# Graph attention and a quantised feed-forward block in one launch: the residual written out early, the last products added by the DMA, SiLU in one instruction, two weight rows loaded sooner

## The chip, the cores and the metric

The kernel runs on one core of a Trainium2 chip, in one launch. The metric is the device time of the launch in microseconds (us). Engines are named as in the profile: PE (TensorE), DVE (VectorE), ACT (ScalarE), POOL (GpSimd), SP (SyncE, which here only issues DMAs).

## The reference

`x` is 384 x 1024, float32. The reference computes two residual blocks:

```python
x = x + GNN(layernorm(x))      # q,k,v = Linear; q2,k2,v2 = inner Linear of each; 16 heads of 64
                               # softmax(q2 k2^T / 8 + edge mask) v2, then Linear wo
x = x + FFN(layernorm(x))      # below

def FFN(x):                                   # 1024 -> 352 -> 1024
    xq   = fake_quant(x, clip_x)              # scale = sigmoid(clip) * max|x| / 127, over the WHOLE tensor
    gate = xq @ fq(w_gate).T                  # fq: int8 rows, scale = max|row| / 127
    up   = xq @ fq(w_up).T
    h    = fake_quant(silu(gate) * up, clip_down)   # again one scale for the whole tensor
    return h @ fq(w_down).T
```

The two maxima over a whole tensor are barriers: nothing can be quantised before the last element of the tensor is known.

## The kernel before, in words

The activations lie transposed in SBUF (features on the 128 partitions), in 8 blocks of 128 features. The work has these stages, with the profile's times from the start of the span:

1. **0 to 23 us**: load `x`, layernorm, transpose, first q columns. Edge lists become keys; POOL scatters edge weights into a mask in DRAM with 51 indirect DMAs until about 160 us.
2. **23 to 161 us**: `project2` (L178 to L226) makes q, k, v and the inner q with 7 block products instead of 8 per pair of output blocks, each of 4 matmuls (L189). One call is a round of some 9.1 us. DVE combines the products (L200 to L221) and prepares the weights of the next round (`left_sums`, L162 to L176; L171 makes `s2`, which the second product of the next round reads). `aside` feeds DVE one more piece after each product.
3. **161 to 318 us**: eight head pairs. In each, scores (L614), softmax on DVE and ACT (L620, L624, L634), transposes (L644), weighting by v (L652); between them PE takes work that doesn't depend on them: inner k and v, later the output projection.
4. **318 to 345 us**: output projection (L825), residual (`residual`, L757), second layernorm (`normalise`, L767), transposes (L866). The third block of 128 rows is the last; its row maxima go through `all_max` (L127, a transpose on PE and a reduction on DVE) into one scale (`act_scale`, L846).
5. **345 to 373 us**: quantise to int8 and back to bf16 (L894 to L897), gate and up matmuls (L906), SiLU (L912 to L918), maxima (L920), second scale (L930 to L933), quantise (L940 to L945), down products (L954, L958), residual and output (L962 to L967).

`ffn_weights` (L518) is a generator that loads, quantises and transposes the FFN weights, 14 rows of blocks. Two rows are loaded ahead; each step quantises one (L507 reduction, L508, L510, L513 on ACT, L515) and stops at its `yield`; the loop over head pairs takes one step at given places (`prepare`, L712). Its first step comes in `p = 0`.

**What sets the order.** PE, SP and POOL run in the order in which the code issues (`manual_schedule`, L74). DVE and ACT are in written order inside stages 1 and 2 (L266) and from L748 on; between them a scheduler places their instructions from its own estimates. Each engine executes in order, so an instruction that waits holds all behind it. SP's queue before the change, around stage 2's end: two `wik` rows, `biv_b` (L497), two `wiv` (L581), three `w_gate` rows (L528), then `w_up` rows that wait until ACT has freed a row buffer (`rows`, 3 buffers).

`keep_busy(n)` (L868) issues n transposes into a tile that nobody reads; it stands before each wait of PE in stages 4 and 5 (14, 14, 17 of them).

Of the kernel before, what the change touches and what calls it, by code (L numbers as in the profile page):

```python
# [23 lines left out]
F32 = mybir.dt.float32  # L24
# [8 lines left out]
P = 128  # L33
# [28 lines left out]
def gnn_ffn_kernel(ctx: ExitStack, tc: tile.TileContext, a: dict, out: bass.AP):  # L62
# [74 lines left out]
    mask = ffn.tile([P, NT, N], F32)  # L137
    nc.gpsimd.memset(mask, NO_EDGE)
    sig = ffn.tile([P, 2], F32)

    ident_b = const.tile([P, P], BF16)
    later = ph1.tile([P, GROUP * P], F32, name="later", bufs=1)
# [103 lines left out]
    with ph1_stack:  # L246
# [219 lines left out]
        for i, (name, o) in enumerate(todo[:-1]):  # L466
            (wa, wb), sums = wq_next, sums_next
            right, dst, cols = work[name]

            if name == "wq" and o == FIRST:  # L470
                aside = tables()
            elif name == "wiq" and o == KC - 2:
                aside = k_steps
            else:
                aside = islice(groups, GROUP + 1)
            wq_next = [load_w(todo[i + 1][0], todo[i + 1][1] + j) for j in range(2)]
            sums_next, steps = left_sums(*wq_next, turned if todo[i + 1][0] == "wik" else ph1)
            if name == "wv" and o == KC - 4:
                q_right, q_steps = right_sums(qT, ph1, "right")
                work["wiq"] = (q_right, q2, bias_of(3))  # L480
            if name == "wv" and o >= KC - 4:
                steps = in_turn(steps, islice(q_steps, 4))
            if name == "wiq" and o == KC - 4:
                k_right, k_steps = right_sums(kT, turned, "k_right")
                steps = in_turn(steps, islice(k_steps, 4))
            aside = in_turn(aside, steps)
            run(project2(
                wa, wb, sums, right, dst[:, o], dst[:, o + 1], cols[:, o : o + 1], cols[:, o + 1 : o + 2], ps_p, "p",
                lambda: next(aside, None),
            ))  # L490
            run(aside)
            if i == 0:
                nc.scalar.activation(sig, clip, AF.Sigmoid)
        run(groups)


    nc.sync.dma_start(biv_b, row_bcast(a["L0_gnn_biv"], F))  # L497
    ffn_w = ctx.enter_context(tc.tile_pool(name="ffn_w", bufs=1))
    wgT = ffn_w.tile([P, KC, I], BF16)
    wuT = ffn_w.tile([P, KC, I], BF16)  # L500
# [17 lines left out]
    def ffn_weights():  # L518

        units = [(name, m, ic) for m, name in enumerate(("L0_ffn_w_gate", "L0_ffn_w_up")) for ic in range(3)]  # L520
        units += [("L0_ffn_w_down", 2, c) for c in range(KC)]
        ahead = []

        def load_row():
            name, m, j = units[len(ahead)]
            i0, rows = ICS[j] if m < 2 else (j * P, P)
            wn = rows_p.tile([P, F], F32, name="row")
            nc.sync.dma_start(wn[:rows, : F if m < 2 else I], a[name][i0 : i0 + rows, :])  # L528
            ahead.append(wn)

        load_row()
        load_row()
        for u, (name, m, j) in enumerate(units):
            wn = ahead[u]
            if len(ahead) < len(units):
                load_row()
            if m < 2:
                i0, rows = ICS[j]
                wT = (wgT, wuT)[m]
                wq = quantise_rows(wn, rows, F, w_scale[:rows, m, j : j + 1])  # L540
                yield
                pt = ps_tp.tile([P, KC, P], BF16, name="tp")
                for k in range(KC):
                    nc.tensor.transpose(pt[:, k, :rows], wq[:rows, k * P : (k + 1) * P], ident_b[:rows, :rows])
                nc.scalar.copy(wT[:, :, i0 : i0 + rows], pt[:, :, :rows])
            else:
                wq = quantise_rows(wn, P, I, wd_scale[:, j : j + 1])
                yield
                pt = ps_tp.tile([P, 3, P], BF16, name="tp")
                for ic, (i0, rows) in enumerate(ICS):  # L550
                    nc.tensor.transpose(pt[:rows, ic, :], wq[:, i0 : i0 + rows], ident_b)
                nc.scalar.copy(wdT[:, 0:2, j * P : (j + 1) * P], pt[:, 0:2, :])
                nc.scalar.copy(wdT[:96, 2, j * P : (j + 1) * P], pt[:96, 2, :])

    with ExitStack() as ph:
        at = ph.enter_context(tc.tile_pool(name="at", bufs=4))
# [113 lines left out]
                    return  # L670

        NP = H // 2
        prep = ffn_weights()

        k2_next, first = inner_k(0)
        run(first)
# [90 lines left out]
        def normalise(t, last, st, hi, lo):  # L767
# [9 lines left out]
            nc.vector.tensor_scalar(above, hi[:, last : last + 1], hi[:, 0:1], mean, op0=ALU.max, op1=ALU.subtract)  # L777
            below = small.tile([P, 1], F32, name="below")
            nc.vector.tensor_scalar(below, lo[:, last : last + 1], lo[:, 0:1], mean, op0=ALU.min, op1=ALU.subtract)
            far = small.tile([P, 1], F32, name="far")  # L780
            nc.vector.tensor_scalar(far, below, -1.0, above, op0=ALU.mult, op1=ALU.max)

            r0 = small.tile([P, 1], F32, name="r2")
            nc.vector.reciprocal(r0, s0)
# [6 lines left out]
            if t == 0:  # L791
                nc.vector.tensor_mul(row_max[:, 0:1], far, rstd)
            else:
                nc.vector.tensor_scalar(
                    row_max[:, t : t + 1], far, rstd, row_max[:, t - 1 : t], op0=ALU.mult, op1=ALU.max
                )
            if t < NT - 1:

                minus = small.tile([P, 1], F32, name="minus")
                nc.vector.tensor_scalar(minus, mean, -1.0, None, op0=ALU.mult)  # L800
            for g in range(2):
                gs = slice(g * 512, (g + 1) * 512)
                if t < NT - 1:
                    nc.scalar.activation(xn[:, t, gs], x[:, t, gs], AF.Identity, bias=minus)
                    nc.scalar.activation(xn[:, t, gs], xn[:, t, gs], AF.Copy, scale=rstd)
                else:
                    nc.vector.tensor_scalar(xn[:, t, gs], x[:, t, gs], mean, rstd, op0=ALU.subtract, op1=ALU.mult)


        for t in range(NT):  # L810
# [7 lines left out]
            for g, (c0, width) in enumerate(groups):  # L818
# [11 lines left out]
                if 0 < g < len(groups) - 1:  # L830
                    nc.vector.tensor_tensor(hi[:, 0:1], hi[:, 0:1], hi[:, g : g + 1], op=ALU.max)
                    nc.vector.tensor_tensor(lo[:, 0:1], lo[:, 0:1], lo[:, g : g + 1], op=ALU.min)
            normalise(t, len(groups) - 1, st, hi, lo)
        run(prep)


    with ExitStack() as ph:
# [5 lines left out]
        hmx = small.tile([P, 4], F32, name="hmx")  # L843
        nc.gpsimd.memset(hmx, 0.0)

        def act_scale(mx, which):  # L846

            s = small.tile([P, 1], F32, name=f"as{which}")
            nc.vector.tensor_scalar(s, mx, sig[:, which : which + 1], 1.0 / QMAX, op0=ALU.mult, op1=ALU.mult)
            r = small.tile([P, 1], F32, name=f"ar{which}")  # L850
            nc.vector.reciprocal(r, s)
            return s, r

# [18 lines left out]
        turn(0)  # L874
        turn(1)
        keep_busy(14, ps_x, "x")

        idle = small.tile([P, 1], F32, name="idle")
        nc.scalar.activation(idle, clip[:, 0:1], AF.Sigmoid)
        sx, rx = act_scale(all_max(row_max[:, NT - 1 : NT], pt[:, :P]), 0)  # L880
        turn(2)
        keep_busy(14, ps_x, "x")
        gu_scale = small.tile([P, 2, 3], F32, name="gu_scale")
# [8 lines left out]
        for g in range(2):  # L892
            for t in range(2):
                nc.scalar.activation(part(x8, t, g), xnT[t][g], AF.Copy, scale=rx)  # L894
            nc.vector.tensor_scalar(part(x8, 2, g), xnT[2][g], rx, None, op0=ALU.mult)
            for t in (0, 2, 1):
                nc.vector.tensor_copy(part(xqT, t, g), part(x8, t, g))  # L897

        for col, ic, c0, width in ((0, 0, 0, N), (1, 1, 0, N), (2, 2, 0, N // 2), (3, 2, N // 2, N // 2)):
            i0, rows = ICS[ic]  # L900
            cs = slice(c0, c0 + width)
# [2 lines left out]
            for k in range(KC):  # L904
# [3 lines left out]
                    )  # L908
            sg = gu_scale[:rows, 0, ic : ic + 1]
            su = gu_scale[:rows, 1, ic : ic + 1]  # L910
            sgm = ff.tile([P, N], F32, name="sgm", bufs=2)
            nc.scalar.activation(sgm[:rows, :width], pg[:rows, :width], AF.Sigmoid, scale=sg)  # L912
            sl = ff.tile([P, N], F32, name="sl")
            nc.vector.scalar_tensor_tensor(
                sl[:rows, :width], pg[:rows, :width], sg, sgm[:rows, :width], op0=ALU.mult, op1=ALU.mult
            )
            nc.vector.scalar_tensor_tensor(
                hT[:rows, ic, cs], pu[:rows, :width], su, sl[:rows, :width], op0=ALU.mult, op1=ALU.mult  # L918
            )
# [8 lines left out]
            nc.scalar.copy(wd_scale_b[:, g * 512 : (g + 1) * 512], pt.rearrange("p a b -> p (a b)"))  # L928
        keep_busy(17, ps_x, "x")
        mx = small.tile([P, 1], F32, name="hmax")  # L930
        nc.vector.tensor_reduce(mx, hmx, axis=AX.X, op=ALU.max)
        pt = ps_tp.tile([P, P], F32, name="tp")
        sh, rh = act_scale(all_max(mx, pt), 1)  # L933

        h8 = ff.tile([P, 3, N], I8, name="h8", bufs=1)
        hq = ff.tile([P, 3, N], BF16, name="hq", bufs=1)
# [6 lines left out]
        for t in range(NT):  # L943
            ts = slice(t * P, (t + 1) * P)
            nc.vector.tensor_copy(hq[:, :, ts], h8[:, :, ts])  # L945
        last = []
        for t in range(NT):
            ts = slice(t * P, (t + 1) * P)
            for g in range(2):
# [6 lines left out]
                    )  # L956
                y = ff.tile([P, 512], F32, name="y", bufs=6)
                nc.vector.scalar_tensor_tensor(y, pm, sh, wd_scale_b[:, gs], op0=ALU.mult, op1=ALU.mult)  # L958
                if t * 2 + g >= 3:
                    last.append((t, gs, y))  # L960
                else:
                    nc.gpsimd.tensor_add(y, x[:, t, gs], y)  # L962
                    nc.sync.dma_start(out[t * P : (t + 1) * P, gs], y)

        for t, gs, y in last:
            nc.vector.tensor_add(y, x[:, t, gs], y)
            nc.sync.dma_start(out[t * P : (t + 1) * P, gs], y)  # L967


# [45 lines left out]
```

## Time and profile before

| | us |
|---|---|
| three runs | 373.28, 375.11, 375.08 (median 375.08) |
| the profiled execution | 374.68 |
| its span, first to last instruction | 372.9 |
| around the span | 1.78 |
| busy in the span: PE | 357.2 (96%) |
| DVE | 260.5 (70%) |
| ACT | 113.3 (30%) |
| POOL | 73.0 (20%) |
| TensorE clock granted, mean | 0.995 |

All times inside the kernel are counted from the span's start. "Idle before" in brackets is how long the engine stood before the instruction, and what released it. Matmul starts follow each other faster than their durations, since matmuls overlap. DMA rates are those of all 16 DMA engines of the core together.

### The profile page before, as it was taken

To read this page: it belongs to the slowest core of one execution; us is meant where nothing else is said; L and a number is where in the kernel's file an instruction comes from. 1 tells how busy PE (TensorE), PEld (TensorE's weight loads), DVE (VectorE), ACT (ScalarE), POOL (GpSimd) and SP (SyncE) were. 2 spreads that over 40 slices of the span, in tenths; PEclk is the share of its full clock that TensorE was granted. 3 is DMA by queue.
4 is the path that set the end of the run, shared out by engine and by line. 5 is a ranking of instruction groups with operands and counts; after the bars stand their busy time and mean duration, and the time that the engine had idled before them with its cause. 6 is when DMAs were issued, how large, how long until landed. Compare 5 with 4: busy or idle time off the path is not lost.

```text
span 372.9 us, 5877 instructions
## 1 busy us (share of the span) xinstructions
PE 357.2 (96%) x2112; PEld 298.4 (80%) x2113; DVE 260.5 (70%) x788; ACT 113.3 (30%) x270; POOL 73.0 (20%) x81
## 2 busy tenths in 40 slices
PE   7999999999999999899999999999999999999971
PEld 6999999999999999797886869687776545449660
DVE  5788888888889986998497367727583530199685
ACT  2242000000000000224573555536443524034330
POOL 6010354455445554300000000000000000000003
PEclk9999999999999999999999999999999999999998
DMA  7969433343333358257260040130394000000004
GB/s 232 394 221 394 135 115 113 116 134 114 113 115 114 113 171 253 74 156 233 56 227 3 19 134 19 53 138 0 131 376 130 5 0 2 0 0 3 1 2 169
DMA packets 17805, 44.52 MB, mean 119 GB/s; under 512 B 3262, under 2 KB 8400, under 8 KB 17392
## 3 DMA queue, kind: packets, MB, share of 16 engines
q1 hardware_dynamic: 15104, 39.46, 31.6%
q0 software_dynamic: 2672, 4.68, 4.1%
q8 instruction: 17, 0.28, 0.3%
q14 instruction: 12, 0.10, 0.1%
HBM read 41.91 MB, written 2.21 MB: 118 GB/s over the span
## 4 chain that ended last, share of the span: by engine, by line
PE 79%; DVE 9%; DMA 7%; ACT 2%; issue 1%; SPq 0%; DVEq 0%; ACTq 0%
PE p L189 34%; PE mm L189 8%; PE mm L591 8%; PE tp L644 4%; PE sc L614 3%; PE sc L652 3%; PE mm L662 3%; PE sc L662 3%; PE mm L825 3%; PE mm L306 3%; DMA row<-in_L_ffn_w_down_dram 3%; DMA row<-in_L_ffn_w_gate_dram 2%; DMA wt<-in_wq_dram 2%; PE sc L825 1%; DVE e L634 1%; DVE y L958 1%
## 5 line engine op out<-in xcount | busy, mean ns | idle before, releaser
L436 POOL DMA_INDIRECT mask_d<-value,place x51 | 57.5, 1128 | 64.9 <-DVE place L433 50.1
L189 PE MATMUL p<-actT,wt 128*128 128x192 f32 x360 | 65.8, 326 | 0.0
L189 PEld LDWEIGHTS p<-actT,wt 128*128 128x128 f32 x360 | 59.7, 190 | 0.0
L591 PE MATMUL mm<-wt,actT 128*128 128x256 f32 x192 | 46.1, 384 | 0.0
L591 PEld LDWEIGHTS mm<-wt,actT 128*128 128x128 f32 x192 | 34.8, 190 | 7.8 <-issue 2.2
L624 ACT ACTIVATE e<-s,mn 128x384 f32<-128x384 f32 x48 | 29.0, 606 | 26.8 <-DVE mn L620 26.7
L620 DVE CUSTOM_DVE_ANT_0 s<-sc,mask 128x384 f32<-128x384 f32 x48 | 24.5, 551 | 13.1 <-PE sc L614 13.0
L189 PE MATMUL p<-x_right,s 128*128 128x192 f32 x176 | 32.2, 326 | 0.0
L189 PE MATMUL p<-x_right,wt 128*128 128x192 f32 x176 | 32.2, 326 | 0.0
L842 POOL MEMSET hT<- 128x384 f32 x1 | 0.4, 418 | 156.9 <-PE sc L652 156.9
L189 PEld LDWEIGHTS p<-x_right,wt 128*128 128x128 f32 x176 | 29.2, 190 | 0.0
L189 PEld LDWEIGHTS p<-x_right,s 128*128 128x128 f32 x176 | 29.2, 190 | 0.0
L646 ACT COPY eTs<-tp 128x384 f32<-128x384 f32 x48 | 20.5, 478 | 25.5 <-PE tp L644 25.5
L423 DVE SCALAR_TENSOR_TENSOR junk<-key_b,key,later 128x384 f32<-128x384 f32 (+3 forms) x51 | 27.5, 539 | 0.0
L203 ACT COPY actT<-p 128x192 f32<-128x192 f32 x15 | 4.8, 318 | 66.1 <-PE p L189 66.1
L200 DVE SCALAR_TENSOR_TENSOR actT<-p,bias,actT 128x192 f32<-128x192 f32 x45 | 18.7, 415 | 8.4 <-PE p L189 6.6
L213 ACT ACTIVATE actT<-p,bias 128x192 f32<-128x192 f32 x15 | 6.3, 420 | 52.7 <-PE p L189 52.7
L644 PEld LDWEIGHTS tp<-ident,e 128*128 128x128 f32 x144 | 17.1, 141 | 5.0 <-issue 2.4
L644 PE MATMUL tp<-ident,e 128*128 128x128 f32 x144 | 19.7, 273 | 0.3 <-ACT eTs L646 0.3
L614 PE MATMUL sc<-k,actT 64*128 64x384 f32 x96 | 19.9, 518 | 0.0
L189 PE MATMUL mm<-actT,wt 128*128 128x192 f32 x96 | 18.9, 329 | 0.0
L634 DVE TENSOR_SCALAR e<-e,rs 128x384 f32<-128x384 f32 x48 | 17.2, 415 | 0.4
(215 smaller groups left out, 590.4 us busy)
## 6 DMA issues: line engine op xcount, KB each, us to landing
wt<-in_wq_dram SPq DMA_DIRECT2D x8, 512.0 KB, 11.4
wt<-in_wk_dram SPq DMA_DIRECT2D x8, 512.0 KB, 4.3
wt<-in_wv_dram SPq DMA_DIRECT2D x8, 512.0 KB, 4.3
wt<-in_wiq_dram SPq DMA_DIRECT2D x8, 512.0 KB, 3.9
wt<-in_wik_dram SPq DMA_DIRECT2D x8, 512.0 KB, 4.7
wt<-in_wiv_dram SPq DMA_DIRECT2D x8, 512.0 KB, 5.2
wt<-in_wo_dram SPq DMA_DIRECT2D x8, 512.0 KB, 7.6
actT<-in_x_dram SPq DMA_DIRECT2D x6, 512.0 KB, 4.2
```

Of the source, the lines that this page charges most:

```text
L189: nc.tensor.matmul(z, left[:, k * P : (k + 1) * P], r[:, k, :], start=(k == 0), stop=(k == HK - 1))
L200: nc.vector.scalar_tensor_tensor(dst, z, b, with_, op0=ALU.add, op1=ALU.add)
L423: nc.vector.scalar_tensor_tensor(junk[:, :left], keys[:, (c - k0) * P : (c - k0) * P + left], key[:, c : c + 1], later[:, :left], op0=ALU. ...
L436: ins = nc.gpsimd.indirect_dma_start(out=mask_d, out_offset=bass.IndirectOffsetOnAxis(ap=place[:, c : c + 1], axis=0), in_=value[:, c : c ...
L591: nc.tensor.matmul(pm, vT[:, k, t * P : (t + 1) * P], wt[k // HK][:, k0 : k0 + 256], start=(k == 0), stop=(k == KC - 1),)
L614: nc.tensor.matmul(ps[t, h], q2[hs, t * P : (t + 1) * P], k2[hs, :], start=True, stop=True)
L620: nc.vector.tensor_tensor_reduce(s, ps[t, h], mask[:, t, :], -SCALE, 3.0e38, op0=ALU.add, op1=ALU.min, accum_out=mn[h][:, t : t + 1],)
L624: nc.scalar.activation(e[h][:, t, :], s, AF.Exp, bias=mn[h][:, t : t + 1], scale=-1.0, accum_out=sm[h][:, t : t + 1],)
L634: nc.vector.tensor_scalar(e[h][:, t, :], e[h][:, t, :], rs[:, t : t + 1], None, op0=ALU.mult)
L644: nc.tensor.transpose(pt[:, t * P : (t + 1) * P], e[h][:, t, m * P : (m + 1) * P], ident)
L646: nc.scalar.copy(eT[h][m], pt)
L662: nc.tensor.matmul(pm, outT[:, k, t * P : (t + 1) * P], wo[k][:, gs], start=(k == 0), stop=(k == KC - 1))
```

## The change

Four parts; the names are those of the code.

- **FFN rows ahead of `wiv`**: a `yield` after the first two `load_row()`; the generator is made and advanced once before the head pairs, ahead of the load of `biv_b`. SP's queue becomes `wik`, `wik`, `w_gate` rows 1 and 2, `biv_b`, `wiv`, `wiv`, `w_gate` row 3. The scheduler places the first two reductions of gate rows about one round sooner on DVE.
- **Scales**: sigmoid(clip)/127 is made once on ACT, early (`per_max`), and multiplied into the row maxima in `normalise` (`size`, `far`) and, for the second scale, into the final reduction (`tensor_tensor_reduce` instead of `tensor_reduce`). `act_scale` goes: what `all_max` returns is the scale, and one reciprocal follows.
- **Last row block and SiLU**: of the third block, columns 0 to 511 are normalised on DVE after `row_max`, columns 512 to 1023 on ACT in two instructions. Of its two quantisations, one moves from DVE to ACT. `Sigmoid` on ACT and a product on DVE become one `Silu` on ACT, four times; the table load for it moves behind the quantisation.
- **Output**: SP writes `x` after the first residual to the output, six DMAs of 128 x 512, as soon as each part is final. The six additions (three on POOL, three on DVE) go; each product `y` is sent by POOL's queue with `accumulate add` onto the output.

```diff
@@ first round of project2
                 nc.scalar.activation(sig, clip, AF.Sigmoid)
+                nc.scalar.activation(per_max[:, 0:1], sig[:, 0:1], AF.Copy, scale=1.0 / QMAX)
+                nc.scalar.activation(
+                    per_max[:, 1:5], sig[:, 1:2].to_broadcast([P, 4]), AF.Copy, scale=1.0 / QMAX
+                )
...
-    nc.sync.dma_start(biv_b, row_bcast(a["L0_gnn_biv"], F))
@@ ffn_weights
         load_row()
         load_row()
+        yield
...
+    prep = ffn_weights()
+    next(prep)
+    nc.sync.dma_start(biv_b, row_bcast(a["L0_gnn_biv"], F))
...
-        prep = ffn_weights()
@@ normalise
+            size = small.tile([P, 1], F32, name="size")
+            nc.vector.tensor_scalar(size, below, -1.0, above, op0=ALU.mult, op1=ALU.max)
             far = small.tile([P, 1], F32, name="far")
-            nc.vector.tensor_scalar(far, below, -1.0, above, op0=ALU.mult, op1=ALU.max)
+            nc.vector.tensor_mul(far, size, per_max[:, 0:1])
+            if t == NT - 1:
+                minus = small.tile([P, 1], F32, name="minus")
+                nc.vector.tensor_scalar(minus, mean, -1.0, None, op0=ALU.mult)
...
-            for g in range(2):
+            for g in range(2) if t < NT - 1 else (1,):
                 gs = slice(g * 512, (g + 1) * 512)
-                if t < NT - 1:
-                    nc.scalar.activation(xn[:, t, gs], x[:, t, gs], AF.Identity, bias=minus)
-                    nc.scalar.activation(xn[:, t, gs], xn[:, t, gs], AF.Copy, scale=rstd)
-                else:
-                    nc.vector.tensor_scalar(xn[:, t, gs], x[:, t, gs], mean, rstd, op0=ALU.subtract, op1=ALU.mult)
+                nc.scalar.activation(xn[:, t, gs], x[:, t, gs], AF.Identity, bias=minus)
+                nc.scalar.activation(xn[:, t, gs], xn[:, t, gs], AF.Copy, scale=rstd)
+            return mean, rstd
@@ first scale
-        idle = small.tile([P, 1], F32, name="idle")
-        nc.scalar.activation(idle, clip[:, 0:1], AF.Sigmoid)
-        sx, rx = act_scale(all_max(row_max[:, NT - 1 : NT], pt[:, :P]), 0)
+        nc.vector.tensor_scalar(
+            xn[:, NT - 1, :512], x[:, NT - 1, :512], mean, rstd, op0=ALU.subtract, op1=ALU.mult
+        )
+        sx = all_max(row_max[:, NT - 1 : NT], pt[:, :P])
+        rx = small.tile([P, 1], F32, name="ar0")
+        nc.vector.reciprocal(rx, sx)
@@ quantise
-            nc.vector.tensor_scalar(part(x8, 2, g), xnT[2][g], rx, None, op0=ALU.mult)
-            for t in (0, 2, 1):
+            if g == 0:
+                nc.vector.tensor_scalar(part(x8, 2, g), xnT[2][g], rx, None, op0=ALU.mult)
+            else:
+                nc.scalar.activation(part(x8, 2, g), xnT[2][g], AF.Copy, scale=rx)
+            for t in ((2, 0, 1), (0, 1, 2))[g]:
                 nc.vector.tensor_copy(part(xqT, t, g), part(x8, t, g))
+        idle = small.tile([P, 1], F32, name="idle")
+        nc.scalar.activation(idle, clip[:, 0:1], AF.Silu)
+        for t in range(NT):
+            for g in range(2):
+                gs = slice(g * 512, (g + 1) * 512)
+                nc.sync.dma_start(out[t * P : (t + 1) * P, gs], x[:, t, gs])
@@ SiLU
-            nc.scalar.activation(sgm[:rows, :width], pg[:rows, :width], AF.Sigmoid, scale=sg)
...
-            nc.vector.scalar_tensor_tensor(
-                sl[:rows, :width], pg[:rows, :width], sg, sgm[:rows, :width], op0=ALU.mult, op1=ALU.mult
-            )
+            nc.scalar.activation(sl[:rows, :width], pg[:rows, :width], AF.Silu, scale=sg)
@@ second scale
-        nc.vector.tensor_reduce(mx, hmx, axis=AX.X, op=ALU.max)
+        nc.vector.tensor_tensor_reduce(
+            scaled, hmx, per_max[:, 1:5], 1.0, -3.0e38, op0=ALU.mult, op1=ALU.max, accum_out=mx
+        )
...
-        sh, rh = act_scale(all_max(mx, pt), 1)
+        sh = all_max(mx, pt)
+        rh = small.tile([P, 1], F32, name="ar1")
+        nc.vector.reciprocal(rh, sh)
@@ output
-                if t * 2 + g >= 3:
-                    last.append((t, gs, y))
-                else:
-                    nc.gpsimd.tensor_add(y, x[:, t, gs], y)
-                    nc.sync.dma_start(out[t * P : (t + 1) * P, gs], y)
-        for t, gs, y in last:
-            nc.vector.tensor_add(y, x[:, t, gs], y)
-            nc.sync.dma_start(out[t * P : (t + 1) * P, gs], y)
+                nc.gpsimd.dma_start(out[ts, gs], y, accum_op=ALU.add)
```

More of the change, by code (lines that the diff above doesn't have):

```diff
@@ L139, in gnn_ffn_kernel @@
     sig = ffn.tile([P, 2], F32)
+    per_max = ffn.tile([P, 5], F32)
     ident_b = const.tile([P, P], BF16)
@@ L832, in gnn_ffn_kernel @@
                     nc.vector.tensor_tensor(lo[:, 0:1], lo[:, 0:1], lo[:, g : g + 1], op=ALU.min)
-            normalise(t, len(groups) - 1, st, hi, lo)
+            mean, rstd = normalise(t, len(groups) - 1, st, hi, lo)
         run(prep)
@@ L844, in gnn_ffn_kernel @@
         nc.gpsimd.memset(hmx, 0.0)
[L846 to L852, printed above, removed]
         pt = ps_x.tile([P, 512], F32, name="x")
@@ L910, in gnn_ffn_kernel @@
             su = gu_scale[:rows, 1, ic : ic + 1]
-            sgm = ff.tile([P, N], F32, name="sgm", bufs=2)
-            nc.scalar.activation(sgm[:rows, :width], pg[:rows, :width], AF.Sigmoid, scale=sg)
             sl = ff.tile([P, N], F32, name="sl")
-            nc.vector.scalar_tensor_tensor(
-                sl[:rows, :width], pg[:rows, :width], sg, sgm[:rows, :width], op0=ALU.mult, op1=ALU.mult
-            )
+            nc.scalar.activation(sl[:rows, :width], pg[:rows, :width], AF.Silu, scale=sg)
             nc.vector.scalar_tensor_tensor(
@@ L930, in gnn_ffn_kernel @@
         mx = small.tile([P, 1], F32, name="hmax")
-        nc.vector.tensor_reduce(mx, hmx, axis=AX.X, op=ALU.max)
+        scaled = small.tile([P, 4], F32, name="hscaled")
+        nc.vector.tensor_tensor_reduce(
+            scaled, hmx, per_max[:, 1:5], 1.0, -3.0e38, op0=ALU.mult, op1=ALU.max, accum_out=mx
+        )
         pt = ps_tp.tile([P, P], F32, name="tp")
-        sh, rh = act_scale(all_max(mx, pt), 1)
+        sh = all_max(mx, pt)
+        rh = small.tile([P, 1], F32, name="ar1")
+        nc.vector.reciprocal(rh, sh)
         h8 = ff.tile([P, 3, N], I8, name="h8", bufs=1)
@@ L945, in gnn_ffn_kernel @@
             nc.vector.tensor_copy(hq[:, :, ts], h8[:, :, ts])
-        last = []
         for t in range(NT):
```

## The prediction

> **What bounds the kernel now.** I read the shares first, then the chain of waits, then the timeline around each place that the diff touches.
>
> ```profile
> PE 357.2 (96%) x2112; PEld 298.4 (80%) x2113; DVE 260.5 (70%) x788; ACT 113.3 (30%) x270; POOL 73.0 (20%) x81
> ```
>
> PE is busy 96% of the span, so up to 345 us only what makes PE stand still can be won. PE's own timeline between 100 and 345 us has three stops of over 0.3 us: 1.80 at 153.22, 0.52 at 192.16, 0.33 at 279.00. The largest, on PE and on DVE:
>
> ```profile
> 147.92 1.22 DVE L507 TENSOR_REDUCE wmx<-row 128x1 f32<-128x1024 f32 x1 [1.55 <-DMA row<-in_L_ffn_w_gate_dram]
> ...
> 150.54 1.22 DVE L507 TENSOR_REDUCE wmx<-row 128x1 f32<-128x1024 f32 x1 [0.28 <-DMA row<-in_L_ffn_w_gate_dram]
> ...
> 152.48 0.68 DVE L171 TENSOR_TENSOR s<-s,wt 128x512 f32<-128x512 f32 x1
> ...
> 153.22 1.57 PE L189 MATMUL p<-right,s 128*128 128x192 f32 x8 [1.80 <-DVE s L171]
> ```
>
> DVE stood for two gate rows, L171 behind them came late, and PE stood for L171. In the last stage the chain of waits goes over DVE and PE in turn, and ends so:
>
> ```profile
> 356.63 0.87 PE tp L927 x8
> 357.51 1.85 PE x L872 x17
> 359.36 0.14 PE tp L129
> 359.50 0.02 issue
> 359.53 0.30 DVE allmax L131
> 359.83 0.03 issue
> 359.86 0.22 DVE as L849
> ```
>
> The 17 fillers of L872, not the data, release L129 here. After the products the output DMAs remain. The table by stretch has, from 368 us on, the DMA share and GB/s as its last columns:
>
> ```profile
> 368.00:369.00 1.00, 0.00 (x0) 0.00 (x0) 0.47 (x1) 0.00 (x0) 0.00 (x0) 1.00 0.99 377
> 369.00:370.00 1.00, 0.00 (x0) 0.00 (x0) 0.00 (x0) 0.00 (x0) 0.00 (x0) 0.68 1.02 387
> 370.00:370.50 0.50, 0.00 (x0) 0.00 (x0) 0.00 (x0) 0.00 (x0) 0.00 (x0) 0.50 0.66 250
> 370.50:372.90 2.40, 0.00 (x0) 0.00 (x0) 0.00 (x0) 0.00 (x0) 0.00 (x0) 0.50 0.00 0
> ```
>
> The engines end at 368.47; the DMAs move data until 370.33 (0.66 of the third row) at 100% share and some 390 GB/s; 2.6 us of closing follow in any case.
>
> **Part 1, FFN rows ahead.** The first two gate rows were issued at 141.48 behind two `wiv` rows. Now they follow the `wik` rows, at about 132.4, where `biv_b` stood. `biv_b` landed 5.5 us after 132.42, at 137.9; gate row 1 takes that place, row 2 needs 512 KB at 390 GB/s more, 1.3 us: 139.2. In the new order of DVE the two reductions stand behind the L423 that ended at 137.41 and behind L218 some 3 us later, so they wait for data at most 0.5 us. They cost DVE the same 2 x 1.22, but a round sooner. I followed DVE's order from there with the durations of before: it runs some 2.5 us behind the old times at 142 us (the four PSUM buffers of L189 and the 3.5 us by which L171 is ahead in that round cover this), catches up in its old gaps, and ends L171 of the last round at 151.8 to 152.3, since gate row 3's reduction (1.20) still stands ahead of it. PE wants it at 151.42. The stop of 1.80 becomes 0.4 to 0.9: 0.9 to 1.4 won, I take 1.1.
>
> `w_up` rows then need not hold SP: the second one kept SP from 154.91 to 164.4, and the next `wik` with it (DVE waited 1.04 for that at 171.10). The third up row's reduction (1.22 at 173.92, between two L620) comes sooner, so the softmax and what follows on ACT are some 0.5 us earlier. That takes something from the stop of 0.52 at 192.16 and from two gaps of 0.18 at 166.50 and 169.39. I take 0.4 of these 0.88. Sum: **-1.5**. Bounds: -2.7 (all of 1.80 and 0.88), and +0.3, if the rows in flight share the DMA engines, gate row 1 lands at 139.5 and DVE carries another 1.6 us into the last round. `biv_b` moves to about 140.7; its reader L597 starts at 176.55. The mask's scatters move by 2 us; the mask is read at 173.24 and was back at 164.5.
>
> **Part 2, up to the first scale.** Each `normalise` gains one small DVE instruction on the way (0.16; by starts 0.2), the last one also `minus`: 0.24. For t = 0 and 1 the idle 0.34 ahead of 341.51 hides all but 0.07. Then only one L807 half (0.50) stands between `row_max` and L131, and L849 (0.24 by starts) goes. By starts, L131 begins at 345.22 instead of 345.30 and the reciprocal ends at 345.70 instead of 346.02. ACT makes the other half in two instructions of 0.72 from about 343.9 on, done at 345.3 to 345.6, when PE has finished the first four transposes. Quantisation started on ACT 0.38 after the reciprocal and is now five instructions at 0.58 by starts on ACT, with the casts behind it: the last cast ends at 349.5 instead of 349.88. PE, filled to 347.9, then runs on from 349.55 instead of 349.93: **-0.35** (bounds 0, if ACT's half is late, and -0.6, if those 0.38 vanish). The table load (1.28 at 343.04) moves behind ACT's quantisation, 349.1 to 350.4; SiLU's first input comes at about 350.9. The cover is 0.5 us; without it the load costs up to 0.8.
>
> **Part 3, SiLU and second scale.** The trace shows no Silu; I take Sigmoid's rows (0.58 and 0.42), same shape and engine. Four DVE products leave (0.62, 0.62, 0.41, 0.41), and the last maximum comes about 1.0 us sooner. That is worth **nothing**: the fillers on PE still end as late. Without the fillers it would be 1.0. The new reduction with its accumulator read (L759 at 128 wide: 0.30) hides there too. Behind L131, L849 leaves the path: **-0.24**. All products `y` are then 0.6 us earlier: the first ends at 362.3, the sixth at 365.6.
>
> **Part 4, output.** Off the path go three DVE additions (L966, 2.35 together) and three on POOL (1.27 each). The early writes are six DMAs on SP, whose queue is empty from 286.4 on; they start between 326 and 342 us, where the DMA engines move nothing, and land (2.1 us) 18 us ahead of the first addition. They cost nothing. The accumulating DMAs are issued by POOL, each behind its `y`. An issue on POOL takes 0.54 (L257) to 0.80 (L450), about the 0.66 between two `y`; from L450's issue to its first data were 1.5 us. First data: 362.3 + 0.1 + 1.5 = 363.9. Then six transfers at a price p each, which no row shows:
>
> - p = 0.67, a plain write (256 KB at 390 GB/s): end 367.9, against 370.33: -2.4. Less is excluded, as the write rows are at full share.
> - p = 1.34, if fetching the old output costs as much as a second transfer: end 371.9, +1.6.
> - p = 2.1, if each waits for the landing of the one before (the output's row, issue to landing): end 376.5, +6.2.
>
> The write row is the nearest, but its engines are at 100%, so the second read can't be free; reading and writing overlap in a plain DMA, so it need not cost all. I take 1.0, between the first two: end 369.9, **-0.4**.
>
> A page speaks against the change here. "Collectives: The Full Stack" of the Trainium skill, section "The bandwidth ceiling: the fold count and why AG ≠ RS ≠ AR", says that an addition inside a DMA reads two sources through the ring that limits it, and gives a measured ratio of 1.93 between plain and adding transfers. By that estimate p is 1.29 and the sum comes to 374.5. No run here shows it yet.
>
> **Sum.** Against the profiled execution, 374.68 (span 372.9 + 1.78): -1.5 from part 1, -0.4 from part 4, in which the 0.35 + 0.24 of parts 2 and 3 are contained: **372.8**. That execution lies 0.40 below the median of the three runs, 375.08.
>
> **Rivals.**
> - *The write price holds* (p = 0.67): -1.5 - 2.4, 370.8. For it: the DMA engines are idle until then, and the price is that of the rows at hand. Against it: full share with one read. Chance 0.25.
> - *The DMA takes back what the engines won* (p = 1.2 to 1.5): 374.0 to 375.8, at 1.34 374.8. POOL's and DVE's additions went, but the bytes that are read double. Chance 0.22.
> - *Slower: the additions in the DMA go one after the other.* Place: the 16 DMA engines after 363.9. Price: at p = 2.1, +6.2 - 1.5, 379.4. It ties at p = 1.32 and is slower by over 0.5% (377.0) from 1.70. For it: nothing else may touch a destination between its read and write. Against it: each DMA is 128 separate rows over 16 engines, which need not wait for each other. Chance 0.08.
> - *The gate rows don't land in time* (part 1 worth +0.3 to -0.5): 373.8 to 374.6. Against it: rows in one queue landed one after another here (6.4, 8.5, 8.6 us after issue). Chance 0.05.
>
> **Numbers.** The forecast, p of 0.85 to 1.2 with part 1 as taken, has 0.40. The range goes from 370.5 (write price, part 1 at -1.8) to 375.9 (p = 1.34, part 1 at -0.4). A measurement here tells about 0.5% from no change, that is 373.2 and 377.0: the first rival and three quarters of the forecast lie below, 0.56; the serial rival and the end of the second above, 0.12; 0.32 between.
>
> **What would show it.** Part 1: PE's stop at 153 is under 1 us, and the gate rows' reductions on DVE wait for no DMA. Part 2: the first scale's reciprocal 0.3 earlier against the end of the last residual. Part 3: fillers still run into the transpose of `all_max` with DVE idle before its reduction. Part 4: the DMA share stays near 1 after the last `y`; six transfers divided by that time give p. I am wrong if p is outside 0.85 to 1.2, if POOL's issues are over 0.66 apart, or if Silu or its table load delays the first maximum.

## The result and the profile after

| | before | after |
|---|---|---|
| median of 4 runs, us | 375.1 | 380.61 |
| ratio, 95% interval | | 1.0152 (1.0122 to 1.0182) |
| profiled execution | 374.68 | 380.61 |
| its span | 372.9 | 378.9 |
| first `y` ends | 362.91 | 362.52 |
| first output data | 365.10 | 364.35 |
| last output data (but for single packets, up to 370.4 and 374.6) | 370.33 | 374.4 |
| from there to the end of the span | 2.6 | 4.5 |

The forecast was 372.8, in a range of 370.5 to 375.9. The kernel became 1.5% slower. The shares of the profile after:

```profile
PE 358.7 (95%) x2112; PEld 298.9 (79%) x2113; DVE 255.0 (67%) x782; ACT 115.6 (31%) x275; POOL 78.0 (21%) x84
```

DVE works 5.5 us less and PE 1.5 us more: the engines do not show the loss. The table by stretch of the kernel after does (length, then busy time of PE, PEld, DVE, ACT, POOL; PE's clock, DMA share and GB/s):

```profile
364.00:366.00 2.00, 0.99 (x5) 0.25 (x3) 1.81 (x3) 0.00 (x0) 2.00 (x4) 1.00 0.85 95
366.00:368.00 2.00, 0.00 (x0) 0.00 (x0) 0.00 (x0) 0.00 (x0) 2.00 (x3) 1.00 1.15 180
368.00:370.00 2.00, 0.00 (x0) 0.00 (x0) 0.00 (x0) 0.00 (x0) 0.28 (x1) 1.00 1.08 118
370.00:372.00 2.00, 0.00 (x0) 0.00 (x0) 0.00 (x0) 0.00 (x0) 0.00 (x0) 0.54 1.05 175
372.00:374.00 2.00, 0.00 (x0) 0.00 (x0) 0.00 (x0) 0.00 (x0) 0.00 (x0) 0.50 1.11 202
374.00:374.50 0.50, 0.00 (x0) 0.00 (x0) 0.00 (x0) 0.00 (x0) 0.00 (x0) 0.50 0.37 62
374.50:378.90 4.40, 0.00 (x0) 0.00 (x0) 0.00 (x0) 0.00 (x0) 0.00 (x0) 0.50 0.00 0
```

The DMA engines are full (share near 1 or above, as packets overlap), but move 95 to 202 GB/s where the plain writes moved some 390. Six blocks of 256 KB in the 10.05 us from 364.35 to 374.4 are 1.7 us each. The rate is not even: it is low until 366, and again, at 118 GB/s with full engines, from 368 to 370. Then 4.5 us pass in which no engine and no DMA works. The end of the timeline after:

```profile
361.77 0.75 DVE L976 SCALAR_TENSOR_TENSOR y<-mm,allmax,wd_scale_b 128x512 f32<-128x512 f32 x1 [0.27 <-PE mm L972]
...
362.83 5.45 POOL L978 DMA_DIRECT2D out_dram<-y  x6 [16.40 <-DVE y L976]
```

The first `y` ends at 361.77 + 0.75 = 362.52, only 0.39 sooner than before. POOL needs 5.45 us for six issues, 0.91 each.

At the second maximum the order is as predicted. Fillers and transpose on PE, maximum and next reduction on DVE, from the timeline after:

```profile
357.21 2.02 PE L878 MATMUL x<-ident 128*128 128x128 f32 x17
...
357.83 0.08 DVE L946 DVE_READ_ACCUMULATOR2_ANT hmax<- 128x1 f32 x1
359.07 0.27 PE L129 MATMUL tp<-ident,hmax 128*128 128x128 f32 x1
359.38 0.29 DVE L131 TENSOR_REDUCE allmax<-tp 128x1 f32<-128x128 f32 x1 [1.47 <-PE tp L129]
```

SiLU brings the maximum to 357.9, and DVE then stands 1.47 us until the 17 fillers let the transpose go. SiLU's table load delays nothing: it ends at 350.59, and the first SiLU on ACT, at 351.20, has waited 0.39 for PE. Around the FFN rows, the first two reductions on DVE, L172 on DVE, and PE's stops of over 0.3 us in the kernel after:

```profile
138.99 1.22 DVE L512 TENSOR_REDUCE wmx<-row 128x1 f32<-128x1024 f32 x1 [1.50 <-DMA row<-in_L_ffn_w_gate_dram]
141.38 1.21 DVE L512 TENSOR_REDUCE wmx<-row 128x1 f32<-128x1024 f32 x1
152.04 0.68 DVE L172 TENSOR_TENSOR s<-s,wt 128x512 f32<-128x512 f32 x1
```

```profile
148.18 1.57 PE L190 MATMUL p<-actT,wt 128*128 128x192 f32 x8 [0.42 <-issue]
152.78 1.57 PE L190 MATMUL p<-right,s 128*128 128x192 f32 x8 [0.43 <-DVE s L172]
158.77 1.57 PE L190 MATMUL p<-actT,wt 128*128 128x192 f32 x8 [0.53 <-DVE wt L211]
167.21 1.57 PE L190 MATMUL mm<-k_right,wt 128*128 128x192 f32 x8 [0.37 <-DVE k L201]
```

The stop of 1.80 is 0.43 now. Three others of this size stand beside it that were not there: 0.42, 0.53 and 0.37.

To tell the stages apart over several traces I use four landmarks: PE in steady rounds near 100 us (100.55 in the kernel before), PE's first `wiv` products (170.79), the first transposes of the third block (341.31), and the start of the first `y` (362.16).

### The profile page after: what moved, and what is told of

It reads as the page before. It is cut to its first block, busy times and chain, and to the rows that moved or that the text cites. A ratio compares the mean times of both kernels' runs of the same rounds, so it can differ in the third digit from the quotient of the medians.

```text
span 378.9 us, 5878 instructions
## 1 busy us (share of the span) xinstructions
PE 358.7 (95%) x2112; PEld 298.9 (79%) x2113; DVE 255.0 (67%) x782; ACT 115.6 (31%) x275; POOL 78.0 (21%) x84
## 4 chain that ended last, share of the span: by engine, by line
PE 63%; issue 14%; DVE 10%; DMA 6%; ACT 3%; POOL 1%; POOLq 0%; SPq 0%; ACTq 0%
PE p L190 29%; PE mm L602 8%; PE mm L190 7%; PE tp L655 4%; PE sc L625 3%; PE sc L663 3%; PE mm L673 3%; PE mm L307 3%; DMA row<-in_L_ffn_w_down_dram 3%; PE sc L673 2%; DMA row<-in_L_ffn_w_gate_dram 2%; DVE wmx L512 1%; DVE e L645 1%; ACT w8b L518 1%; POOL out_dram L978 1%
## 5 line engine op out<-in xcount | busy, mean ns | idle before, releaser
L437 POOL DMA_INDIRECT mask_d<-value,place x51 | 60.8, 1191 | 64.9 <-DVE place L434 45.8
```

Of the source, the lines that this page charges most:

```text
L437: ins = nc.gpsimd.indirect_dma_start(out=mask_d, out_offset=bass.IndirectOffsetOnAxis(ap=place[:, c : c + 1], axis=0), in_=value[:, c : c ...
```

## The experiments

The theory after the result: the adding transfers cost 1.7 us each instead of 1.0, and the way they are sent lengthens the closing. The rivals: the loss comes from another part; or GpSimd's queue, not the addition, is what is slow.

**The output part alone.** The kernel before, with

```diff
+        for t in range(NT):          # ahead of the gate and up products
+            for g in range(2):
+                nc.sync.dma_start(out[t * P : (t + 1) * P, gs], x[:, t, gs])
...
-                    nc.gpsimd.tensor_add(y, x[:, t, gs], y)
-                    nc.sync.dma_start(out[t * P : (t + 1) * P, gs], y)
+                nc.gpsimd.dma_start(out[ts, gs], y, accum_op=ALU.add)
```

and the three additions of `last` gone.

> The kernel before with the output part alone (residual written early, six adding transfers on GpSimd's queue). Theory 1, the adding transfers are what costs: from the kernel after, data moves for 10.1 us after the first y (6 x 1.7) and 4.7 us of closing follow, against 7.4 and 2.6 in the kernel before; y comes 0.4 later than in the kernel after (362.9 against 362.5), so 381.0 us, ratio 1.016. Theory 2, the loss comes from the other parts (a later first y, hidden in my alignment of the two traces): within 1 us of the kernel before, 374 to 376.

Measured: 381.5, ratio 1.0164 (1.0135 to 1.0193). Its first `y` starts 20.87 us after the transposes, against 20.85 before: the early writes delay nothing. Data moves until 375.5, 12.0 us after the first `y` ended (7.4 before), and 4.4 us follow. The whole loss is in the output part. (With full engines, the rate here is 153 to 196 GB/s in each stretch of two microseconds from 366 to 374.)

**The FFN rows alone.**

```diff
-    nc.sync.dma_start(biv_b, row_bcast(a["L0_gnn_biv"], F))
...
         load_row()
         load_row()
+        yield
...
+    prep = ffn_weights()
+
+    next(prep)
+    nc.sync.dma_start(biv_b, row_bcast(a["L0_gnn_biv"], F))
...
-        prep = ffn_weights()
```

> The kernel before with the FFN rows ahead of wiv alone. Theory 1, VectorE is full from 142 to 170 us and now has six of the 1.2 us reductions there instead of five: PE's stop at 153 shrinks but others open at 148, 159 and 167, and PE starts L602's first group 0.5 to 0.7 later than before (171.3 to 171.5 on this scale) and is 0.5 later at 340 us; the span is 0.3 to 0.6 us longer, 375.0 to 375.3 for the profiled execution. Theory 2, my prediction's step: 1.5 shorter, 373.2; then the lateness in the kernel after has another cause, the instructions that the other parts add.

Measured: 374.58, ratio 0.9988 (0.9973 to 1.0003), which is -0.45 us with an interval of -1.0 to +0.1. The predicted -1.5 lies outside, a loss of 0.5 too. PE's stops near 148, 153 and 159 are 0.43, 0.43 and 0.53, as in the kernel after, where the row of the first names no releaser. Here it does:

```profile
148.44 1.57 PE L189 MATMUL p<-actT,wt 128*128 128x192 f32 x8 [0.43 <-DVE wt L210]
```

**The first scale and SiLU alone.** The kernel after, with these taken back:

```diff
-    next(prep)
...
-                nc.sync.dma_start(out[t * P : (t + 1) * P, gs], x[:, t, gs])
...
-                nc.gpsimd.dma_start(out[ts, gs], y, accum_op=ALU.add)
+                    nc.gpsimd.tensor_add(y, x[:, t, gs], y)
+                    nc.sync.dma_start(out[t * P : (t + 1) * P, gs], y)
```

> The kernel before with the shorter way to the first scale and SiLU alone, the output as before. Theory 1: counted from the last residual's start, the first y is 0.95 us sooner than before (19.70 against 20.65 in the two traces), so the profiled execution takes 373.7. Theory 2: y is sooner but the tail is bound by the output transfers, which end no earlier than 370.0: 374.3 or more.

Measured: 373.24, ratio 0.9959 (0.9940 to 0.9978), -1.5 us. From the transposes to the first `y` it takes 19.91 us, against 20.85 to 20.87 in seven traces of kernels without this part (and 20.59 in an eighth): -0.95. Data ends at 370.0 and 2.6 us follow. The output does not bound the end there: what `y` gains is gained.

**Plain writes on GpSimd's queue.**

```diff
-        for t in range(NT):
-            for g in range(2):
-                gs = slice(g * 512, (g + 1) * 512)
-                nc.sync.dma_start(out[t * P : (t + 1) * P, gs], x[:, t, gs])
...
-                nc.gpsimd.dma_start(out[ts, gs], y, accum_op=ALU.add)
+                nc.gpsimd.dma_start(out[ts, gs], y)
```

> The kernel after with six plain writes on GpSimd's queue in place of the adding ones, and without the early writes: the residual is left out of the output. Theory 1, the addition costs: transfers at the price of a write (0.67 each) behind issues, data ends by 369.0, closing 2.6 us, total 373.4. Theory 2, GpSimd's queue costs (its issues are 0.9 us apart and its completion is late): data ends at 370 or later and the closing stays near 4.7, total 376.5 to 380.

Measured: 374.35, ratio 0.9992 (0.9973 to 1.0011). Its last stretches:

```profile
364.00:366.00 2.00, 0.00 (x0) 0.00 (x0) 0.53 (x1) 0.00 (x0) 1.12 (x3) 1.00 0.94 346
366.00:367.50 1.50, 0.00 (x0) 0.00 (x0) 0.00 (x0) 0.00 (x0) 0.00 (x0) 1.00 0.83 314
367.50:372.00 4.50, 0.00 (x0) 0.00 (x0) 0.00 (x0) 0.00 (x0) 0.00 (x0) 0.51 0.00 0
```

Each theory has half. The data goes at 346 GB/s in the full stretch and ends at 367.4, 6.2 us after the first `y` ended (11.9 in the kernel after): the addition makes the transfers slow. But 4.6 us of closing follow here too, without any addition: that belongs to the queue. POOL's six issues take 3.83 us, 0.64 each, the pitch of the `y`.

**One adding transfer, at the end.** The kernel before, block 6 sent as in the kernel after:

```diff
+        nc.sync.dma_start(out[2 * P :, 512:], x[:, 2, 512:])
...
+                if t * 2 + g == 5:
+                    nc.gpsimd.dma_start(out[ts, gs], y, accum_op=ALU.add)
+                elif t * 2 + g >= 3:
-                if t * 2 + g >= 3:
                     last.append((t, gs, y))
```

> The kernel before, but its last block is sent with the addition on GpSimd's queue, its residual written early; the other five go as before. In the plain writes on that queue the closing after the last data was 4.6 us, in the kernel before 2.6. Theory 1, the longer closing belongs to GpSimd's queue at the end and not to the addition or to the number of transfers: data of the one transfer from about 368 to 369.5, closing 4.6, span 374 to 374.5, total about 376 (1.003). Theory 2, the closing grows with the additions still open: closing under 3.5, span 372 to 373, total 374 to 375.

Measured: 376.99, ratio 1.0082 (1.0056 to 1.0109). 3.4 us follow the last data, between the theories. But two of SP's writes end last here, at 370.5; the adding transfer is through at about 370, some 4 us before the end. This run alone doesn't decide it.

**Wider rows.** The kernel after, with each product in one half of a `y` of 128 x 1024:

```diff
-                y = ff.tile([P, 512], F32, name="y", bufs=6)
+                if g == 0:
+                    y = ff.tile([P, F], F32, name="y", bufs=3)
...
-                nc.gpsimd.dma_start(out[ts, gs], y, accum_op=ALU.add)
+            nc.gpsimd.dma_start(out[ts, :], y, accum_op=ALU.add)
```

> The kernel after with three adding transfers of 128 x 1024 in place of six of 128 x 512. The six used 768 data packets of 2 KB for 10.1 us, the plain writes on the same queue 384 of 4 KB for 4.6. Theory 1, a packet has its price and its size little: rows of 4 KB give half the packets, data moves for 5 to 6 us, and although the first transfer waits for the second y (0.7), the total is 3 to 4 us below the kernel after, 376.5 to 377.5. Theory 2, the price goes by the byte that is read and written: again 8 to 10 us of data, total 379.5 to 381.5.

Measured: 379.81, ratio 1.0153 (1.0128 to 1.0179), and its last stretches:

```profile
364.00:366.00 2.00, 0.60 (x3) 0.10 (x1) 1.42 (x3) 0.00 (x0) 1.24 (x3) 1.00 0.74 94
366.00:368.00 2.00, 0.00 (x0) 0.00 (x0) 0.00 (x0) 0.00 (x0) 0.57 (x1) 0.73 1.08 203
368.00:370.00 2.00, 0.00 (x0) 0.00 (x0) 0.00 (x0) 0.00 (x0) 0.00 (x0) 0.50 1.05 186
370.00:372.00 2.00, 0.00 (x0) 0.00 (x0) 0.00 (x0) 0.00 (x0) 0.00 (x0) 0.50 1.08 213
```

Half the packets, in half as many transfers, and nearly the same total: the data takes 8.6 us (364.6 to 373.2) in place of 10.05, so most of the price goes by the byte. The packet size is not what makes it slow: SP's plain writes in the kernel before also went in packets of 2 KB, at some 390 GB/s. The best stretches here move 203 and 213 GB/s, which is 1.29 and 1.23 us for 256 KB. Until 366 it is about 134 GB/s (94 over two microseconds, of which data moves in 1.4); this and slower stretches between lift the mean to 8.6 / 6 = 1.43.

**SiLU with fewer fillers.** The run with the first scale and SiLU alone, with

```diff
-        keep_busy(17, ps_x, "x")
+        keep_busy(7, ps_x, "x")
```

> The run with the first scale and SiLU alone, with 7 fillers on TensorE ahead of the second maximum's transpose in place of 17. Theory 1, what SiLU saves on VectorE was hidden by the fillers (VectorE stood 1.46 us for that transpose): ten fillers of 0.109 us less bring the transpose and all behind it forward by 1.0 us, 372.3 (0.993). Theory 2, the fillers keep TensorE's granted clock or the output's transfers bound the end: the same as with 17, 373.2.

Measured: 372.14, ratio 0.9944 (0.9927 to 0.9961).

```profile
355.68 0.93 PE L874 MATMUL x<-ident 128*128 128x128 f32 x7
356.29 0.08 DVE L938 DVE_READ_ACCUMULATOR2_ANT hmax<- 128x1 f32 x1
...
356.85 0.29 DVE L131 TENSOR_REDUCE allmax<-tp 128x1 f32<-128x128 f32 x1 [0.48 <-PE tp L129]
```

DVE's wait for the transpose falls from 1.46 to 0.48, and from the transposes to the first `y` it takes 18.91 us, 1.00 less. The granted clock stays 1.00 up to the output.

**One adding transfer, at the start.** The kernel before, block 1 sent as in the kernel after.

```diff
+        nc.sync.dma_start(out[:P, :512], x[:, 0, :512])
...
+                if t * 2 + g == 0:
+                    nc.gpsimd.dma_start(out[ts, gs], y, accum_op=ALU.add)
+                elif t * 2 + g >= 3:
-                if t * 2 + g >= 3:
                     last.append((t, gs, y))
```

> The kernel before, but its first block is sent with the addition on GpSimd's queue, its residual written early; GpSimd adds two blocks, VectorE three, as before, and these five go by SyncE's queue. Theory 1, the longer closing is the wait for the completion of the last transfers on GpSimd's queue: the one here is complete before the end, closing 2.6, total 374 to 375.5. Theory 2, it is there as soon as the program has used that queue for output at all: closing 4.6, total 376.5 to 377.5.

Measured: 374.75, ratio 1.0013 (0.9991 to 1.0035). The transfer that stands alone, and the end:

```profile
365.00:367.00 2.00, 0.81 (x4) 0.19 (x2) 2.00 (x4) 0.00 (x0) 2.00 (x2) 1.00 0.94 137
...
370.00:371.00 1.00, 0.00 (x0) 0.00 (x0) 0.00 (x0) 0.00 (x0) 0.00 (x0) 0.50 0.78 297
371.00:373.40 2.40, 0.00 (x0) 0.00 (x0) 0.00 (x0) 0.00 (x0) 0.00 (x0) 0.50 0.00 0
```

Alone it takes 2.0 us, from 365.2 to 367.2, which is some 131 GB/s (the row holds a few of SP's packets too). SP's writes end at 370.8 and 2.6 us follow, as before: a transfer of GpSimd's queue that is long over lengthens nothing.

**The last block by GpSimd's queue, plain.**

```diff
-            nc.sync.dma_start(out[t * P : (t + 1) * P, gs], y)
+            q = nc.gpsimd if t * P + gs.start == 2 * P + 512 else nc.sync
+            q.dma_start(out[t * P : (t + 1) * P, gs], y)
```

> The kernel before, but its last block, already added up by VectorE, is written by GpSimd's queue instead of SyncE's; nothing is added in a transfer. After the last data of GpSimd's queue the closing was 4.3 to 4.6 us in four traces, after that of SyncE's 2.6. Theory 1, the queue alone makes this: closing 4.0 or more and some 2 us over the kernel before, 376 to 377 (1.004 to 1.007). Theory 2, one plain transfer is closed as fast as any: closing 2.6 to 3, 374 to 375.5.

Measured: 377.01, ratio 1.0070 (1.0038 to 1.0101), +2.6 us.

```profile
370.50:371.00 0.50, 0.00 (x0) 0.00 (x0) 0.00 (x0) 0.00 (x0) 0.00 (x0) 0.50 0.55 213
...
373.00:375.80 2.80, 0.00 (x0) 0.00 (x0) 0.00 (x0) 0.00 (x0) 0.00 (x0) 0.50 0.00 0
```

Data ends at 371.0, 4.8 us before the end. One plain write on that queue, if it is the last, costs the whole longer closing.

**Shorter maxima of the FFN rows.** The run with the rows alone, with

```diff
-    def quantise_rows(wn, rows, n, scale):
+    def quantise_rows(wn, rows, n, scale, of=None):
...
-        nc.vector.tensor_reduce(mx[:rows], wn[:rows, :n], axis=AX.X, op=ALU.max, apply_absolute_value=True)
+        nc.vector.tensor_reduce(mx[:rows], wn[:rows, : of or n], axis=AX.X, op=ALU.max, apply_absolute_value=True)
...
-                wq = quantise_rows(wn, rows, F, w_scale[:rows, m, j : j + 1])
+                wq = quantise_rows(wn, rows, F, w_scale[:rows, m, j : j + 1], 352)
```

> The run with the FFN rows ahead alone, but the maximum of the six gate and up rows is taken over their first 352 of 1024 columns, so that each of these reductions costs VectorE about 0.52 us instead of 1.21 (the rest of the maximum is left out). Theory 1, VectorE is full there, so that the rows ahead only exchange one stop of TensorE for several: 4.1 us less on VectorE takes away most of the stops of 0.43, 0.43 and 0.53, and TensorE reaches the first group of wiv products 1 us sooner or more, counted from 100 us (three traces each: 70.2 to 71.0 in the old order, 70.4 to 70.8 in the new); 0.995 to 0.997 of the kernel before. Theory 2, the stops come from loads that land late (rows or weights): they stay, and the time too, 0.999.

Measured: 372.71, ratio 0.9932 (0.9906 to 0.9958). PE has no stop of over 0.3 us between 130 and 180 us, and goes from 100 us to the first `wiv` products in 67.93 us, against 70.39 with full maxima, and 70.4 to 70.8 in four other traces of the new order. DVE's load by stretches of ten microseconds (DVE, clock, DMA share, GB/s), first with the rows alone, then with short maxima:

```profile
146.00:156.00 10.00, 10.00 (x26) 1.00 0.69 222
156.00:166.00 10.00, 9.41 (x25) 1.00 0.33 91
```

```profile
146.00:156.00 10.00, 10.00 (x33) 1.00 0.85 260
156.00:166.00 10.00, 7.82 (x21) 1.00 0.50 153
```

The first short reduction still waits 1.00 for its row, and the stops are gone all the same: they come from DVE's load, not from late loads.

**Fewer fillers without SiLU.** The kernel before, with

```diff
-        keep_busy(17, ps_x, "x")
+        keep_busy(7, ps_x, "x")
```

> The kernel before with 7 fillers in place of 17 ahead of the second maximum's transpose. Theory 1, without SiLU the maximum itself is ready only 0.15 us before the fillers end, so fewer of them gain at most 0.2 (0.9995), and the 0.9944 of SiLU with 7 fillers needs both. Theory 2, fewer fillers are the whole gain: 1.0 us, 0.997.

Measured: 374.55, ratio 0.9990 (0.9968 to 1.0013). DVE's wait for the transpose is 0.48, as in the kernel before:

```profile
358.19 0.29 DVE L131 TENSOR_REDUCE allmax<-tp 128x1 f32<-128x128 f32 x1 [0.48 <-PE tp L129]
```

From the transposes to the first `y` it is 20.85, to the hundredth as before. The gain needs both.

**Everything but the output part, with 7 fillers.** The kernel after, with the additions on GpSimd and VectorE and SyncE's writes of the kernel before, and

```diff
-        keep_busy(17, ps_x, "x")
+        keep_busy(7, ps_x, "x")
```

> The kernel after with the output part undone (as in the kernel before) and 7 fillers in place of 17 ahead of the second maximum: FFN rows ahead, the shorter way to the first scale and SiLU. Theory 1, the parts add: 0.9944 with SiLU and fewer fillers, 0.9988 for the rows: 0.993, 371.8. Theory 2, the rows ahead give nothing or cost: 372.2 or more.

Measured: 372.34, ratio 0.9930 (0.9902 to 0.9958). It beats both kernels, and so does the run with SiLU and 7 fillers without the rows (0.9944); the two can't be told apart.

## Why the prediction was wrong

Of the 7.8 us between 372.8 and 380.61, 4.05 are the price of the adding transfers (10.05 against 6), 1.9 the closing (4.5 against 2.6), and 1.95 the start of the data: on the forecast's account 362.4 (363.9 less the 1.5 of part 1), measured 364.35. 0.1 goes the other way around the span. In the 1.95, part 1 is 2.06 too late, parts 2 and 3 give back 0.36, and the way from `y` to the first data takes the rest.

- **The price p.** The failed step is "I take 1.0, between the first two". It measured 1.7 in the kernel after (10.05 / 6). The reason that I gave for a price below 1.34, that reading and writing overlap, has nothing for it: even the best stretches, 202 to 213 GB/s, are 1.23 to 1.30 a transfer, little under two full transfers (1.34). And a bound on the best rate was no bound on six transfers at the end of a kernel: up to 366 us data moves at 115 to 134 GB/s, from 368 to 370 at 118 in the kernel after, and one transfer alone takes 2.0. Why the rate is so low in these stretches is not shown. I had called the serial rival (p = 2.1, 379.4) the least likely of the large ones; its number came nearest, but not its mechanism. If the transfers went one after the other, six would take 12.6 us and the rate would not reach 200 GB/s.
- **POOL's issues.** I said about 0.66 apart; they are 0.91 (5.45 / 6) with the addition and 0.64 (3.83 / 6) without. On this queue each 256 KB goes in 128 packets of 2 KB with the addition, in 64 of 4 KB without it. First data came 1.8 us after the first `y`; I had said 1.6.
- **The closing.** "2.6 us of closing follow in any case" failed. It holds where SP's queue moves the last data and GpSimd's has long been done (2.5 to 2.6 in eight traces). Where GpSimd's queue does, 4.3 to 4.8 follow, in five traces, with addition or without, with one transfer or six. What the chip does in that time no row shows; only the place is shown, not the cause.
- **Part 1.** The step "the stop of 1.80 becomes 0.4 to 0.9" came true (0.43), and it was not worth 1.1: the third block's transposes start at 341.87 in the kernel after, 0.56 later than before and not 1.5 sooner. The cover that I named, four PSUM buffers and 3.5 us of L171, was too little: PE stops at 148 and 159 for DVE instead. DVE is full there (10.00 of 10 us from 146 on), and the change takes no work from it. Two things were not in the one trace I had. The old stop depends on when the first gate row lands; in eight traces of the old order it was 0.45 to 1.84, so 1.80 is its upper end. And the way from 100 us to the first `wiv` products took 68.8 to 71.0 in those eight traces, 70.4 to 70.8 in five of the new order: it became steadier, not shorter (means 69.9 and 70.6). The first reduction waited 1.50 for its row, where I said at most 0.5.
- **Part 2 and 3, on the way to the first `y`.** The mechanism was right and the size too small: 0.35 + 0.24 = 0.59 said, 0.95 measured. Most of the rest comes from the 0.38 between the reciprocal and ACT's first quantisation, which I had kept for the lower bound. In the kernel after the reciprocal ends at 346.19 and ACT starts at 346.29: 0.10.
- **SiLU worth nothing while 17 fillers stand, 1.0 without them**: right, by the two runs with 7 fillers (1.00 with SiLU, 0.00 without). The reading "The 17 fillers of L872, not the data, release L129" does not hold for the kernel before: there the maximum was ready just as the fillers ended, and with 7 fillers the wait is the same 0.48. The fillers hold the transpose only once SiLU is there.
- **Early writes cost nothing**: right (20.87 against 20.85).

The page "Collectives: The Full Stack" of the Trainium skill, section "The bandwidth ceiling: the fold count and why AG ≠ RS ≠ AR", explains its ratio of 1.93 by two reads on one ring; it measured that ratio between two collectives, one that copies and one that adds, over four ranks. The best stretches here agree with the number: 390 GB/s before against 203 to 213 is 1.83 to 1.92. That two reads are the cause here no run shows. The estimate of 1.29 for p that I worked out from it would still have fallen short of the 1.43 and 1.7 over whole sequences.

## What to carry to other kernels

An addition inside a transfer is not free because the DMA engines look idle: at the end of a kernel its price per byte and the closing of the queue that must carry it are both on the path, and here together they cost 6 us to save additions that took 2.35 on DVE. Give a transfer that no row shows at least the price of all its reads and writes, and let a fixed time at the end depend on the queue until rows for that queue show otherwise. A stop that vanishes on a full engine comes back beside it; count that engine's work in the whole stretch before and after, and a gain that waits behind fillers is only had when the fillers go.

## What the runs showed that I had not expected

- Adding transfers from SBUF onto DRAM: 202 to 213 GB/s in the best stretches of 2 us, 115 to 134 GB/s in the first 1.5 us or so, 2.0 us for 256 KB alone; plain writes on the same queue 346 GB/s.
- From the last data to the end of the span: 2.5 to 2.6 us after SP's queue, 4.3 to 4.8 us after GpSimd's.
- The same rounds of unchanged code took 68.8 to 71.0 us in eight traces, and mostly the longer, the longer DVE waited for the first gate rows (0.58 to 2.14 us).
